# Attention, first of eight layers: TensorE's steps taken in groups, late loads cut in pieces, a normalization started earlier

## The chip, the cores and the metric

The kernel runs on one core of a Trainium2 chip. The metric is device microseconds (us) of one execution; the kernel before has a median of 3373.56 us over three runs (3370.95 to 3374.28). TensorE is called PE in the profile, VectorE DVE, ScalarE ACT, GpSimd POOL and SyncE SP.

## The reference, cut to what matters

The model has eight layers; only the first, a causal attention with 16 heads of 64 features on 4 batches of 1024 tokens and 128 features, is touched. All is in float32.

```
q = split_heads(x @ Wq); k = split_heads(x @ Wk); v = split_heads(x @ Wv)
scores = einsum('bhid,bhjd->bhij', q * beta, k)
scores = where(causal, mask_value, scores)
attn = softmax(scores, axis=-1)
out = einsum('bhij,bhjd->bhid', attn, v)
return out @ Wo + bo
...
x = x + _L0_attn_a_ref(_layernorm(x, axis=-1), ...)
```

## The kernel before, in words

Class `AttentionA` does this layer. Two heads make a pair; pair n (0 to 31) is a batch n // 8 and a pair n % 8 in it. The 1024 queries of a pair are cut in four quarters gq = 0 to 3 of 256 queries, that is two row blocks of 128. Work has two stages, which run about half a pair apart.

The first stage, `probabilities` (lines 336 to 391), takes one row block ib of a quarter at a time, in chunks of up to 512 keys. PE makes the scores of both heads (L352: the heads lie in the two halves of the 64-row weights) into a PSUM tile s. DVE adds the mask, negates, moves the chunk to p in SBUF and keeps the running minimum (L358, one instruction per head). After the last chunk ACT takes the exponential of the block in place (L367, one per head) and sums it. After the second block of a quarter DVE takes reciprocals r (L380), SP stores them to DRAM (L383) and loads them back twice, spread over 64 partitions each (L386), as the tile share.

The second stage, `outputs` (L414), works through a quarter in gq + 1 steps of two key blocks. PE turns the blocks of p with 8 transposes (6 in the last, diagonal step) into PSUM tiles t (L426); DVE copies the first key block to SBUF (L433), ACT the second (L431). Then PE multiplies the turned blocks with v into a PSUM tile o (L451); the two heads go to the two halves of its columns. At the end of a quarter DVE multiplies o with share (L458).

What PE does is written in one fixed order (`pe`, a chain of dependencies over all its instructions of the layer), and DVE's masked minima and the normalization are in another (`ve`). In a step of the kernel before the order is: transposes of this step; one entry of the list `pieces`, if there is one; the scores that `ahead` gives (it keeps the first stage 20 units of 128x128 keys per head ahead of the second); the products of the step **before** (the list `waiting`). Pieces are: two transposes of the normalized x per batch (L260), q and k of a pair (four of L280), values of two pairs (four of L291), the product with Wo (two of L318), and at the end of a batch two transposes back (L328). Each takes the one PSUM tile of the pool `a_pm`, and is evacuated by DVE or ACT.

PSUM has eight banks: two tiles s of two banks each, two tiles t of one, one for o, one for the pieces.

`normalized(b)` (L248) does the layernorm of a batch: on DVE 8 `bn_stats`, 8 `bn_aggr`, a reciprocal and 8 subtract-multiply instructions (L117 to L124), on ACT a square root (L121), on POOL the bias added to x (L251); then it puts the two transposes into `pieces`. It is called for batch b at quarter 0 of pair 8b - 2.

`load_late` (L91) defers the two 2 MB loads of the expert weights W1 and W2 of the second layer; they are issued on ACT's queue, with a small exponential of another layer ahead of them, all at once after the first exponentials of quarter 2 of pair 0 (L371 to L377).

Of the kernel before, what the change touches and what calls it, by code (L numbers as in the profile page):

```python
# [11 lines left out]
F32 = mybir.dt.float32  # L12
# [15 lines left out]
DH_A = 64  # L28
# [33 lines left out]
class Kernel:  # L62
# [28 lines left out]
    def load_late(self, pool, name, shape, src):  # L91

        t = pool.tile(shape, F32, name="w_" + name)
        self.late.append(lambda: self.nc.scalar.dma_start(t, src))
        return t

    def broadcast_row(self, pool, name, width):
# [97 lines left out]
class AttentionA:  # L195
# [8 lines left out]

    Q = 2
    NQ = NC // 2
    LEAD = 20

    def __init__(self, k: Kernel):
# [9 lines left out]
    def __call__(self, start=None):  # L221
# [4 lines left out]
        with self.stack as ctx:  # L226
# [1 line left out]
            one = ctx.enter_context(tc.tile_pool(name="a_one", bufs=1))  # L228
            sb = ctx.enter_context(tc.tile_pool(name="a_sb", bufs=2))
            dram = ctx.enter_context(tc.tile_pool(name="a_dram", bufs=6, space=DRAM))  # L230
            ps_s = ctx.enter_context(tc.tile_pool(name="a_ps", bufs=2, space=PSUM))
            ps_t = ctx.enter_context(tc.tile_pool(name="a_pt", bufs=2, space=PSUM))
            ps_o = ctx.enter_context(tc.tile_pool(name="a_po", bufs=1, space=PSUM))
            ps_m = ctx.enter_context(tc.tile_pool(name="a_pm", bufs=1, space=PSUM))
            pe, ve = k.order(), k.order()
# [6 lines left out]
                out=mask[:, MW - P :], in_=mask[:, MW - P :], compare_op=ALU.is_ge, fill=MASKED, base=0,  # L242
                pattern=[[-1, P]], channel_multiplier=1,
            )
            xts, pairs, units = {}, {}, {}
            pieces = []

            def normalized(b):  # L248
                xl = one.tile([P, NC, C], F32, tag="xl", name="xl")
                k.normalize(xl, k.xb(b), pin=ve)  # L250
                nc.gpsimd.tensor_tensor(  # L251
                    k.xb(b), k.xb(b), bo.unsqueeze(1).to_broadcast([P, NC, C]), ALU.add
                )

                def turned(h):
                    if h == 0:
                        xts[b] = one.tile([P, T], F32, tag="xt", name="xt")
                    ps = ps_m.tile([P, 512], F32, tag="m", name="ps")
                    for c in range(4):
                        pe(nc.tensor.transpose(ps[:, c * P : (c + 1) * P], xl[:, h * 4 + c, :], k.ident))  # L260
                    k.evacuate(xts[b][:, h * 512 : (h + 1) * 512], ps)

                pieces.extend([(NP * b, lambda: turned(0)), (NP * b, lambda: turned(1))])
# [72 lines left out]
            def probabilities(n, gq):  # L336
# [7 lines left out]
                for i in range(Q):  # L344
                    ib = gq * Q + i
                    width = (ib + 1) * P
                    for at, lo in enumerate(range(0, width, 512)):
                        hi = min(lo + 512, width)
                        s = ps_s.tile([P, 2, 512], F32, tag="s", name="s")
                        for h in range(2):  # L350
                            feats = slice(h * DH_A, (h + 1) * DH_A)
                            pe(nc.tensor.matmul(  # L352
                                s[:, h, : hi - lo], q[feats, ib * P : (ib + 1) * P], kk[feats, lo:hi],
                                start=True, stop=True,
                            ))
                        m = mask[:, MW - hi + lo :] if hi == width else mask[:, : hi - lo]
                        for h in range(2):
                            ve(nc.vector.tensor_tensor_reduce(  # L358
                                p[:, h, i, lo:hi], s[:, h, : hi - lo], m, -1.0, 3.4e38, ALU.add, ALU.min,
                                tops[:, h, i, at : at + 1],  # L360
                            ))
                        if hi < width:
                            yield (hi - lo) // P
                    if width > 512:
                        nc.vector.tensor_tensor(tops[:, :, i, 0], tops[:, :, i, 0], tops[:, :, i, 1], ALU.min)  # L365
                    for h in range(2):
                        exp = nc.scalar.activation(  # L367
                            p[:, h, i, :width], p[:, h, i, :width], AF.Exp, bias=tops[:, h, i, 0:1],
                            scale=-1.0, accum_out=sums[:, h, i : i + 1],
                        )  # L370
                    if k.late and gq == 2:  # L371
                        pin = k.order()
                        pin(exp)
                        while k.late:
                            pin(k.late.pop(0)())
                        while k.late_v:
                            ve(k.late_v.pop(0)())  # L377
                    if i == Q - 1:
                        r = sb.tile([P, 2, Q], F32, tag="r", name="r")
                        nc.vector.reciprocal(r, sums)  # L380

                        there = dram.tile([2, Q, P], F32, tag="shares", name="shares")
                        nc.sync.dma_start(there.rearrange("h i p -> p h i"), r)  # L383
                        share = sb.tile([P, Q * P], F32, tag="share", name="share", bufs=4)
                        for h in range(2):
                            nc.sync.dma_start(  # L386
                                share[h * DH_A : (h + 1) * DH_A],
                                there[h : h + 1].rearrange("h i p -> h (i p)").to_broadcast([DH_A, Q * P]),
                            )
                        units[n, gq] = p, share  # L390
                    yield (hi - lo) // P
# [17 lines left out]
                    else:  # L409
                        break  # L410

            waiting = []

            def outputs(n, gq):  # L414


                p, share = units.pop((n, gq))
                last = (gq + 1) * Q - 1
                for step in range(gq + 1):
                    products = []  # L420
                    for jb in (2 * step, 2 * step + 1):
                        lo = max(0, jb * P - gq * Q * P)
                        t = ps_t.tile([P, 2, Q * P], F32, tag="t", name="t")
                        for h in range(2):
                            for i in range(lo // P, Q):
                                pe(nc.tensor.transpose(  # L426
                                    t[:, h, i * P : (i + 1) * P], p[:, h, i, jb * P : (jb + 1) * P], k.ident
                                ))
                        pt = sb.tile([P, 2, Q * P], F32, tag=f"pt{jb % 2}", name="pt")
                        if jb % 2:  # L430
                            nc.scalar.copy(pt[:, :, lo:], t[:, :, lo:])  # L431
                        else:
                            nc.vector.tensor_copy(pt[:, :, lo:], t[:, :, lo:])  # L433
                        products.append((jb, lo, pt))
                    done[1] += 4 if step < gq else 3
                    if pieces:
                        pieces.pop(0)[1]()
                    ahead()
                    while waiting:
                        waiting.pop(0)()  # L440
                    if step == 0:
                        o = ps_o.tile([P, Q * P], F32, tag="o", name="o")
                    waiting.append(
                        lambda products=products, step=step: product(n, gq, o, share, products, last, step == gq)
                    )

            def product(n, gq, o, share, products, last, at_end):
                for jb, lo, pt in products:
                    for h in range(2):
                        feats = slice(h * DH_A, (h + 1) * DH_A)  # L450
                        pe(nc.tensor.matmul(  # L451
                            o[feats, lo:], pairs[n]["v"][:, jb, feats], pt[:, h, lo:],
                            start=jb == 0, stop=jb == last,
                        ))
                if at_end:
                    if gq == 0:
                        pairs[n]["o"] = sb.tile([P, T], F32, tag="ot", name="ot")
                    nc.vector.tensor_tensor(  # L458
                        pairs[n]["o"][:, gq * Q * P : (gq + 1) * Q * P], o, share, ALU.mult
                    )  # L460

            normalized(0)
            projected(0)
            projected(1)
            ahead()
            for n in range(B * NP):
                for gq in range(NQ):
                    if gq == 0 and n + 2 < B * NP and (n + 2) % NP == 0:
                        normalized((n + 2) // NP)
                    if gq == 1 and n > 0:  # L470
                        joined(n - 1)
                    if gq == 3 and n + 2 < B * NP:
                        projected(n + 2)
                    outputs(n, gq)
            while waiting:
                waiting.pop(0)()
            joined(B * NP - 1)
            while pieces:
                pieces.pop(0)[1]()
# [1354 lines left out]
```

## Time and profile before

| | us |
|---|---|
| median of three runs | 3373.56 |
| the profiled execution | 3378.53 |
| its span, first to last instruction | 3376.7 |
| first layer: first transpose of probabilities to last product with Wo | 31.96 to 1223 |
| PE busy over the span | 3015.2 (89%) |
| DVE busy | 2306.0 (68%) |
| ACT busy | 1812.9 (54%) |
| mean granted PE clock | 0.947 |

The page gives, for each engine, the time in which it worked; groups of instructions by line; and a chain of waits. In the timeline each row is a run of like instructions: start, length, engine, line, what is written from what, number. A matrix product in float32 is two instructions there, a transpose one. Lengths of PE rows overlap by the time a result is under way, so the distance from one row's start to the next row's start is what PE takes for it.

### The profile page before, as it was taken

The numbers are of one execution on the slowest core, as the hardware profiler recorded it, in microseconds if no ns is written. First come the engines' busy times: TensorE is split into PE (matmuls) and PEld (weight loads), VectorE is DVE, ScalarE is ACT, GpSimd is POOL, SyncE is SP. The second block draws the span as 40 slices with busy tenths as digits, with TensorE's granted clock in tenths as the row PEclk, the third lists the DMA queues.
The fourth block names the chain that finished last, engine by engine and source line by source line (L and its number), as shares of the span: only waits on it lengthen the run. The fifth ranks groups of instructions, "written<-read, shape, count | busy, mean of one in ns | idle before, by whom it ended". The sixth has DMA issues, their size and how long they took to land.

```text
span 3376.7 us, 45533 instructions
## 1 busy us (share of the span) xinstructions
PE 3015.2 (89%) x16624; PEld 1655.0 (49%) x16624; DVE 2306.0 (68%) x5281; ACT 1812.9 (54%) x3819; POOL 273.0 (8%) x269
## 2 busy tenths in 40 slices
PE   5999999999999979869988597978778799999988
PEld 2555555555455547635566344444445344444435
DVE  3666666666776656666566589897977677677634
ACT  2555555555555523445423597979654265556662
POOL 1000000000000002530013200000001101010000
PEclk8999999999999989989999798989999699899999
DMA  5110111111110101100001111111111112121100
GB/s 156 16 16 14 15 18 16 14 17 17 14 17 15 15 8 32 53 10 1 0 16 40 53 64 50 57 57 51 63 38 42 34 44 53 31 51 31 30 2 25
DMA packets 149537, 109.35 MB, mean 32 GB/s; under 512 B 91760, under 2 KB 130432, under 8 KB 146880
## 3 DMA queue, kind: packets, MB, share of 16 engines
q1 hardware_dynamic: 128352, 72.84, 9.4%
q0 software_dynamic: 17408, 27.32, 3.3%
q10 hardware_dynamic: 3552, 6.29, 0.6%
q8 instruction: 130, 2.13, 0.4%
q14 instruction: 95, 0.78, 0.1%
HBM read 90.76 MB, written 15.60 MB: 31 GB/s over the span
## 4 chain that ended last, share of the span: by engine, by line
PE 68%; DVE 11%; ACT 8%; DMA 6%; issue 6%; POOL 1%; SPq 0%; DVEq 0%; ACTq 0%; POOLq 0%
PE s L352 8%; PE t L426 8%; PE o L451 8%; PE acc L649 4%; PE o L1613 4%; PE acc L1227 4%; PE x L1579 3%; PE ps L280 3%; PE acc L948 3%; PE s L1515 3%; ACT p L1585 3%; DMA shares<-r 2%; ACT hc L1226 2%; DVE st L1214 2%; DVE tops L1524 2%
## 5 line engine op out<-in xcount | busy, mean ns | idle before, releaser
L358 DVE CUSTOM_DVE_ANT_0 p<-s,mask 128x512 f32<-128x512 f32 (+3 forms) x768 | 394.6, 553 | 170.5 <-PE s L352 168.3
L367 ACT ACTIVATE p<-p,tops 128x640 f32<-128x640 f32 (+7 forms) x512 | 391.7, 767 | 146.1 <-DVE tops L365 85.4
L1585 ACT ACTIVATE p<-x 128x512 f32<-128x512 f32 (+3 forms) x768 | 337.6, 490 | 246.4 <-PE x L1584 176.6
L1524 DVE TENSOR_REDUCE tops<-s 128x2 f32<-128x1024 f32 (+3 forms) x384 | 361.3, 956 | 133.8 <-PE s L1520 94.2
L431 ACT COPY pt<-t 128x512 f32<-128x512 f32 (+1 forms) x320 | 157.7, 493 | 380.0 <-PE t L426 379.5
L1227 PE MATMUL acc<-hc,ident 128*128 128x512 f32 x512 | 270.1, 652 | 93.2 <-ACT hc L1226 92.3
L352 PE MATMUL s<-kt,qt 64*128 64x512 f32 (+3 forms) x1536 | 339.4, 533 | 2.7 <-DVE tops L358 2.6
L451 PE MATMUL o<-pt,vv 128*64 128x256 f32 (+1 forms) x2560 | 323.3, 374 | 14.7 <-ACT pt L431 9.4
L426 PE MATMUL t<-ident,p 128*128 128x128 f32 x2304 | 326.2, 282 | 3.7 <-DVE pt L433 3.0
L426 PEld LDWEIGHTS t<-ident,p 128*128 128x128 f32 x2304 | 248.1, 142 | 103.3 <-issue 70.0
L1214 DVE TENSOR_TENSOR_SCAN st<-decay,st 128x1024 f32<-128x1024 f32 x128 | 288.8, 2279 | 10.9 <-ACT decay L1211 10.4
L451 PEld LDWEIGHTS o<-pt,vv 128*64 128x64 f32 x2560 | 156.6, 137 | 263.9 <-issue 157.3
L433 DVE COPY pt<-t 128x512 f32<-128x512 f32 x320 | 220.0, 687 | 66.0 <-PE t L426 66.0
L1579 PE MATMUL x<-q,k 75*128 75x512 bf16 (+3 forms) x768 | 223.1, 338 | 27.7 <-ACT p L1585 15.0
L1515 PE MATMUL s<-k,q 72*128 72x512 bf16 (+3 forms) x768 | 216.3, 348 | 31.9 <-DVE tops L1524 17.6
L1226 ACT ACTIVATE hc<-ps,by_time 128x256 f32<-128x256 f32 x512 | 200.7, 478 | 50.6 <-PE ps L1220 50.5
L352 PEld LDWEIGHTS s<-kt,qt 64*128 64x128 f32 x1536 | 112.5, 188 | 180.7 <-issue 139.7
L1227 PEld LDWEIGHTS acc<-hc,ident 128*128 128x128 f32 x512 | 91.7, 198 | 209.6 <-ACT hc L1226 191.0
L738 POOL DMA_INDIRECT got<-y_rows,rows x128 | 136.7, 1068 | 645.1 <-DMA y_rows<-y 543.5
L1213 DVE TENSOR_TENSOR st<-du,bs 128x1024 f32<-128x1024 f32 x128 | 151.8, 1217 | 49.4 <-PE ps L1220 49.2
L649 PE MATMUL acc<-d,xl 128*128 128x480 f32 (+1 forms) x384 | 152.8, 559 | 26.2 <-DVE d L644 26.2
L1220 PEld LDWEIGHTS ps<-ident,st 128*128 128x128 f32 x1024 | 126.0, 146 | 96.5 <-issue 60.7
(272 smaller groups left out, 4740.7 us busy)
## 6 DMA issues: line engine op xcount, KB each, us to landing
bs<-b_rows SPq DMA_DIRECT2D x64, 512.0 KB
share<-shares SPq DMA_DIRECT2D x256, 64.0 KB
k<-b_parts POOLq DMA_DIRECT2D x16, 576.0 KB, 13.2
q<-b_parts POOLq DMA_DIRECT2D x48, 192.0 KB, 12.1
b_parts<-part SPq DMA_DIRECT2D x24, 256.0 KB
y_rows<-y SPq DMA_DIRECT2D x16, 192.0 KB
x<-in_x_dram SPq DMA_DIRECT2D x4, 512.0 KB
w_W<-in_W_dram ACTq DMA_DIRECT2D x1, 2048.0 KB
```

Source lines behind the costliest of these rows:

```text
L352: pe(nc.tensor.matmul(s[:, h, : hi - lo], q[feats, ib * P : (ib + 1) * P], kk[feats, lo:hi], start=True, stop=True,))
L358: ve(nc.vector.tensor_tensor_reduce(p[:, h, i, lo:hi], s[:, h, : hi - lo], m, -1.0, 3.4e38, ALU.add, ALU.min, tops[:, h, i, at : at + 1],))
L367: exp = nc.scalar.activation(p[:, h, i, :width], p[:, h, i, :width], AF.Exp, bias=tops[:, h, i, 0:1], scale=-1.0, accum_out=sums[:, h, i : ...
L426: pe(nc.tensor.transpose(t[:, h, i * P : (i + 1) * P], p[:, h, i, jb * P : (jb + 1) * P], k.ident))
L451: pe(nc.tensor.matmul(o[feats, lo:], pairs[n]["v"][:, jb, feats], pt[:, h, lo:], start=jb == 0, stop=jb == last,))
L649: pe(nc.tensor.matmul(acc[n][:, :m, :].rearrange("p e s -> p (e s)"), xl[:, c, :], d[:, e : e + m, :].rearrange("p e s -> p (e s)"), start ...
L1214: nc.vector.tensor_tensor_scan(st, decay, st, 0.0, ALU.mult, ALU.add)
L1227: nc.tensor.matmul(acc[:, c : c + 2, :].rearrange("p c d -> p (c d)"), k.ident, hc.rearrange("p c d -> p (c d)"), start=n == 0, stop=n == ...
L1515: start.pin(nc.tensor.matmul(s[:, a, : hi - lo], qq[:ROWS, two + a, ib * P : (ib + 1) * P], kk[:ROWS, two + a, lo:hi], start=True, stop=ha ...
L1524: nc.vector.tensor_reduce(tops[:, half, two : two + 2, n], s[:, :, : hi - lo], AX.X, ALU.max)
L1579: start.pin(nc.tensor.matmul(x[:, lo:], kk[:FULL, a, jb * P : (jb + 1) * P], qq[:FULL, a, hq * 512 + lo : (hq + 1) * 512], start=True, sto ...
L1585: nc.scalar.activation(p[:, a, lo:], x[:, lo:], AF.Exp)
```

## The change

Three edits in the first layer.

1. The late loads are cut along the second dimension: W1 and W2 in eight pieces of 256 KB each. Instead of all at once they are issued one per quarter, after the last exponential of the quarter, from quarter 2 of pair 0 on (the small exponential takes the first turn).
2. `normalized` for a batch is called half a pair earlier, at quarter 2 of pair 8b - 3; the two transposes (`across`) are put into `pieces` where they were, at quarter 0 of pair 8b - 2.
3. `outputs` works in groups of steps: quarter 0 has one group of one step, quarter 1 one of two, quarter 2 one of three, quarter 3 two of two. In a group the order is: a piece; all transposes of the group's steps; a piece; the scores that `ahead` gives; the products of this same group. `waiting` is gone. The tiles t of a step are one tile of two banks, taken from the pool of the scores, which now has three tiles for both; the SBUF copies pt have three buffers each instead of two.

```diff
+    GROUPS = [[(0,)], [(0, 1)], [(0, 1, 2)], [(0, 1), (2, 3)]]
...
-        self.late.append(lambda: self.nc.scalar.dma_start(t, src))
+        self.late.extend(
+            lambda at=at: self.nc.scalar.dma_start(t[:, at], src[:, at]) for at in range(shape[1])
+        )
...
-            ps_s = ctx.enter_context(tc.tile_pool(name="a_ps", bufs=2, space=PSUM))
-            ps_t = ctx.enter_context(tc.tile_pool(name="a_pt", bufs=2, space=PSUM))
+            ps_s = ctx.enter_context(tc.tile_pool(name="a_ps", bufs=3, space=PSUM))
...
-                    if k.late and gq == 2:
+                    if k.late and i == Q - 1 and n * NQ + gq > 1:
                         pin = k.order()
                         pin(exp)
-                        while k.late:
-                            pin(k.late.pop(0)())
+                        pin(k.late.pop(0)())
...
+                o = ps_o.tile([P, Q * P], F32, tag="o", name="o")
+                for steps in self.GROUPS[gq]:
+                    piece()
+                    blocks = [block for step in steps for block in turned(p, gq, step)]
+                    piece()
                     ahead()
-                    while waiting:
-                        waiting.pop(0)()
...
+                    for block in blocks:
+                        product(n, gq, o, *block)
...
+                t = ps_s.tile([P, 2, 2, Q * P], F32, tag="s", name="t")
+                blocks = []
+                for m in range(2):
...
+                    blocks.append((jb, lo, sb.tile([P, 2, Q * P], F32, tag=f"pt{m}", name="pt", bufs=3)))
+                for m, (jb, lo, pt) in enumerate(blocks):
+                    if m:
+                        nc.scalar.copy(pt[:, :, lo:], t[:, m, :, lo:])
+                    else:
+                        nc.vector.tensor_copy(pt[:, :, lo:], t[:, m, :, lo:])
+                done[1] += 4 if step < gq else 3
+                return blocks
...
+                    if gq == 2 and n + 3 < B * NP and (n + 3) % NP == 0:
+                        normalized((n + 3) // NP)
                     if gq == 0 and n + 2 < B * NP and (n + 2) % NP == 0:
-                        normalized((n + 2) // NP)
+                        across((n + 2) // NP)
```

More of the change, by code (lines that the diff above doesn't have):

```diff
@@ L244, in __call__ @@
             )
-            xts, pairs, units = {}, {}, {}
+            xls, xts, pairs, units = [], {}, {}, {}
             pieces = []
@@ L253, in normalized, with across @@
                 )
+                xls.append(xl)
+            def across(b):
+                xl = xls.pop()
                 def turned(h):
@@ L410, in ahead, with piece @@
                         break
-            waiting = []
+            def piece():
+                if pieces:
+                    pieces.pop(0)[1]()
             def outputs(n, gq):
                 p, share = units.pop((n, gq))
[L418 to L437, printed above, removed]
-                    ahead()
-                    while waiting:
-                        waiting.pop(0)()
[L441 to L445, printed above, removed]
@@ L447, in product @@
-            def product(n, gq, o, share, products, last, at_end):
-                for jb, lo, pt in products:
-                    for h in range(2):
[L450 to L460, printed above, removed]
+                o = ps_o.tile([P, Q * P], F32, tag="o", name="o")
@@ new lines, in outputs @@
+                for steps in self.GROUPS[gq]:
+                    piece()
+                    blocks = [block for step in steps for block in turned(p, gq, step)]
+                    piece()
+                    ahead()
+                    for block in blocks:
+                        product(n, gq, o, *block)
+                if gq == 0:
+                    pairs[n]["o"] = sb.tile([P, T], F32, tag="ot", name="ot")
+                nc.vector.tensor_tensor(
+                    pairs[n]["o"][:, gq * Q * P : (gq + 1) * Q * P], o, share, ALU.mult
+                )
@@ new lines, in turned @@
+            def turned(p, gq, step):
+                t = ps_s.tile([P, 2, 2, Q * P], F32, tag="s", name="t")
+                blocks = []
+                for m in range(2):
+                    jb = 2 * step + m
+                    lo = max(0, jb * P - gq * Q * P)
+                    for h in range(2):
+                        for i in range(lo // P, Q):
+                            pe(nc.tensor.transpose(
+                                t[:, m, h, i * P : (i + 1) * P], p[:, h, i, jb * P : (jb + 1) * P], k.ident
+                            ))
+                    blocks.append((jb, lo, sb.tile([P, 2, Q * P], F32, tag=f"pt{m}", name="pt", bufs=3)))
[6 more added lines that the diff above has]
+                return blocks
@@ L462, in __call__, with product @@
+            def product(n, gq, o, jb, lo, pt):
+                for h in range(2):
+                    feats = slice(h * DH_A, (h + 1) * DH_A)
+                    pe(nc.tensor.matmul(
+                        o[feats, lo:], pairs[n]["v"][:, jb, feats], pt[:, h, lo:],
+                        start=jb == 0, stop=jb == (gq + 1) * Q - 1,
+                    ))
             normalized(0)
+            across(0)
             projected(0)
@@ L474, in __call__ @@
                     outputs(n, gq)
-            while waiting:
-                waiting.pop(0)()
             joined(B * NP - 1)
```

## The prediction

> **What bounds the kernel now.** I read the page first, then busy times by stretch, then PE's timeline inside a stretch, then the waits around the stretches that are not full. The stretch 97 to 281 us (pairs 1 to 5) is the first layer in its steady state:
>
> ```profile
> core 0: us, PE busy (x) PEld busy (x) DVE busy (x) ACT busy (x) POOL busy (x), PEclk, DMA share, GB/s
> 31.00:97.00 66.00, 45.27 (x202) 23.21 (x200) 23.23 (x71) 20.45 (x49) 2.35 (x2) 0.77 0.32 85
> 97.00:281.00 184.00, 184.00 (x1145) 98.64 (x1142) 127.19 (x396) 97.56 (x233) 0.00 (x0) 1.00 0.12 16
> ```
>
> PE is busy for all 184 us at full clock, DVE for 69%, ACT for 53%: here PE alone sets the time. In 31 to 97 us it is busy for 45 of 66 us at a clock of 0.77. So two questions decide: what PE spends beyond its products, and what comes next once that is less. PE's timeline, two cycles:
>
> ```profile
> 330.47 1.13 PE L352 MATMUL s<-kt,qt 64*128 64x512 f32 x4
> 331.53 1.08 PE L451 MATMUL o<-pt,vv 128*64 128x256 f32 x8
> 332.54 1.09 PE L426 MATMUL t<-ident,p 128*128 128x128 f32 x8
> 333.47 1.03 PE L291 MATMUL ps<-w_Wv,xt 128*128 128x256 f32 x4
> 334.43 1.13 PE L352 MATMUL s<-kt,qt 64*128 64x512 f32 x4
> 335.49 0.87 PE L451 MATMUL o<-pt,vv 128*64 128x256 f32 x8
> 336.29 1.09 PE L426 MATMUL t<-ident,p 128*128 128x128 f32 x8
> ```
>
> Read start to start. Scores take 1.06 for 512 keys (330.47 to 331.53), 0.63 for 256 (320.08 to 320.71): 0.213 per 128 keys and 0.20 beside it. Two score chunks in a row (512 and 128, 316.12 to 317.40) take 1.28, so the 0.20 comes once per run, not per chunk. Products take 1.01, or 0.80 when the second block is half: the same 0.213, and 0.16 beside. Eight transposes take 0.93, six 0.71: 0.107 each and 0.07 beside. A piece takes 0.95: 0.853 and 0.10. Without a piece transposes to scores is 1.03 (299.94 to 300.97), so 0.17 instead of 0.07 + 0.10. Each cycle scores, products, transposes thus pays **0.53 us for changing from one form of product to the next**.
>
> Does that close? Per pair, scores, transposes and products are 36 units each way: 3 x 7.68. Odd pairs have 10 pieces, even ones 6, of 0.853. With ten cycles: 23.0 + 8.5 + 5.3 = 36.9 odd, 33.5 even. The chain of waits has 37.0 (96.4 to 133.4) and 33.7 (to 167.1). It closes.
>
> **The groups (edit 3).** Ten cycles per pair become five. A piece ahead of the transposes adds a change of form: products to piece is 0.17 (1214.03 to 1215.69, sixteen product instructions worth 1.49), in place of products to transposes, and piece to transposes I take at 0.09, between the 0.07 and 0.10 that like changes cost. Odd pairs have five such pieces, even ones three: saved 5 x 0.53 - 0.45 = 2.20 and 5 x 0.53 - 0.27 = 2.38, that is 4.6 us per two pairs. Over 31 pairs (the last is tail): **-71 us** (0.09 between 0 and 0.2: -82 to -58).
>
> What covered before and is late now? I wrote out the order that the code gives; an odd pair is, with T for the eight or six transposes of a step, S with its units, O for the products of a step:
>
> ```
> gq0: piece T piece S4 O            gq1: piece T T piece S3 S4 O O
> gq2: piece T T T piece S4 S1 S2 S3 O O O
> gq3: piece T T piece S4 S4 O O     piece T T piece S1 S4 S2 O O
> ```
>
> (a) Four scores in a row in gq2 meet three PSUM tiles: S3 needs the tile of S4. When DVE gives it back, DVE's timeline shows for a chunk of 512 whose row on PE starts at 614.82:
>
> ```profile
> 615.99 0.69 DVE L358 CUSTOM_DVE_ANT_0 p<-s,mask 128x512 f32<-128x512 f32 x1 [0.29 <-PE s L352]
> 616.61 0.08 DVE L358 DVE_READ_ACCUMULATOR2_ANT tops<- 128x1 f32 x1
> 616.61 0.69 DVE L358 CUSTOM_DVE_ANT_0 p<-s,mask 128x512 f32<-128x512 f32 x1
> 617.22 0.08 DVE L358 DVE_READ_ACCUMULATOR2_ANT tops<- 128x1 f32 x1
> ```
>
> DVE is done 2.48 after the score starts; PE would come back after S4, S1, S2 = 1.49. Stall 1.0 us per pair, with O O O behind it: **+31** (0 if the tiles come free otherwise, +40 if DVE is late besides).
>
> (b) Products wait for their own copies instead of the step before's. DVE's copy is ready about 1.5 us after a step's transposes start (0.75 latency, 0.69). With a piece and scores between, 2 us, it is hidden; that covers all groups but gq0 of even pairs, which has no pieces. And ACT's copy stands behind exponentials in ACT's order:
>
> ```profile
> 613.15 0.87 PE L426 MATMUL t<-ident,p 128*128 128x128 f32 x6
> 613.26 0.94 ACT L367 ACTIVATE p<-p,tops 128x768 f32<-128x768 f32 x1 [2.08 <-DVE tops L365]
> ...
> 615.11 0.35 ACT L431 COPY pt<-t 128x256 f32<-128x256 f32 x1
> ```
>
> The copy ends 2.3 us after these transposes start. Before, nobody was waiting; in gq0 of an even pair the products come 0.81 + 1.06 = 1.9 after, with 0.43 of the first block ahead: some 0.3 late, or 1.2 where the reciprocal (L380; 84.1 us of DVE idle ahead of it in the groups by line, all behind ACT and the stores) holds DVE too. I take 0.65 per two pairs, **+10**; ends 0 and 2 us for every pair, +62.
>
> (c) SP: per pair its stores, waits for landings and loads fill 31.8 of 35.7 us (631.98 to 663.75 of 631.98 to 667.72). A pair will take some 34, so SP still fits; under 31.8 it could not go.
>
> **Normalization (edit 2).** Now transposes stand from 280.40 and the next from 285.07:
>
> ```profile
> 280.40 0.87 PE L426 MATMUL t<-ident,p 128*128 128x128 f32 x6
> 285.07 1.24 PE L260 MATMUL ps<-ident,xl 128*128 128x128 f32 x4 [3.79 <-DVE xl L124]
> 286.24 2.08 PE L352 MATMUL s<-kt,qt 64*128 64x512 f32 x4
> ```
>
> From 280.40 to the scores at 290.81 it is 10.4 us for 4.6 of work; the other two are 11.5 and 10.6: 18.8 us lost in three, part as the wait, part as the half clock after it (scores 2.01 instead of 1.06). Moved, the same 25 DVE instructions (1.65 + 0.62 + 0.20 + 2.14 = 4.6 us), ACT's root with 1.28 of table load before and after, and POOL's 2.35 come in gq2 of an odd pair. In `ve` the masked minima queue behind them, so the next scores' tiles and ACT's exponentials are late: DVE has some 11 us idle per pair but not in one place. I take 3 us for each, bounds 1 and 5: **-10** (-16 to -4). The gaps should stay under those that cost the clock here; a gap of 0.66 (before 315.06) left the next scores at full speed (1.28 for 512 and 128 keys).
>
> **Late loads (edit 1).** 31.96 to 96.31 takes 64.4 us; by the rates above it is 33 of work, so 31 lost. ACT stands until 50.28 with one load of W; PE stands from 44.1 to 53.5 for ACT's copy, then 3.2 for share (before 61.39), behind 4 MB of loads, all followed by half clock:
>
> ```profile
> 50.28 0.02 ACT L94 MOVE_SHAPE w_W<-in_W_dram  x1 [17.23 <-DMA w_b<-in_b_dram]
> ...
> 53.52 0.70 PE L451 MATMUL o<-pt,vv 128*64 128x128 f32 x4 [9.42 <-ACT pt L431]
> ```
>
> In pieces the 17.2 goes. Late next is share of gq0, stored at 36.09: alone, store to load takes 8 to 10 us here, so its product wait ends near 48, some 5 us; the four q and k in a row still wait for their evacuation (2.6 + 0.8 + 0.7). I take 13 left, **-18** (-26, to 0 if a piece's issue waits as the W load did). Sixteen issues of 0.38 to 0.88 us are 6 to 14 us of ACT over 17 quarters, beside 47% idle. The expert weights are needed at 1266 us, after the last piece near 190.
>
> The row says a 2 MB load in one hurt. The Trainium skill, "DMA: Bandwidth & Descriptors", section Bandwidth, says the opposite of cutting: batch to at least 1 MiB. By its fit (2 us fixed, 436 GB/s) sixteen pieces are an estimated 28 us more of transfer than two; were that on the path, the total would be about -28 instead of -56. No row here puts it there.
>
> **Tail.** The last share lands 14 us after its reciprocal (1206.2 to 1220.2) and PE waits 4.4 for it; grouping puts the last scores behind 14 transposes more (1.5 us), and products wait for copies with nothing between: **+2** (0 to +4).
>
> **Sum**: -71 + 31 + 10 - 10 - 18 + 2 = -56. The profiled execution goes from 3378.5 to 3322.5; it lies 5.0 above the median, so the median goes from 3373.6 to **3318**.
>
> **Rivals.** *The stalls do not come* (tiles free in time, copies early): (a) and (b) are 0 and the sum is -97: 3277. For it: DVE has 31% idle. Against: the 2.48 above is a chain, not a load. *The stalls are longer*, by half to all of the 41 of (a) and (b) again (reciprocals that block DVE, SP's rounds, late exponentials): 3338 to 3359, middle 3348. *Slower*: products that wait for their own group's copies at every group, behind exponentials in ACT's queue. It gains 71 + 10 + 18 = 99 without stalls; over 155 groups that is eaten from 0.64 us mean stall per group on; at 0.8 it is +25, 3399. For it: the copy's 2.3 us; against: most groups have a piece and up to four scores there, 2 to 3 us. *The 0.53 is paid per step*, not per change: then grouping saves nothing, the sum is +15, 3389; against it, the two chunks in a row.
>
> **Numbers.** Forecast (3300 to 3334) 0.45; stalls do not come (3262 to 3300) 0.24; longer (3334 to 3366) 0.20; within 0.2% (about 7 us, what a measurement here can tell from no change) 0.03; the two slower ones 0.08. The range takes the forecast, most of the second down to 3268 and of the third up to 3352. Faster 0.89, same 0.03, slower 0.08.
>
> **What would show it.** Steady stretch: two pairs in 68 to 69 us instead of 70.7; fives of cycles per pair; S3 of gq2 released by DVE about 1 us late; a few tenths at gq0 of even pairs; no idle at L260; no 17 us wait at L94. Wrong I would be if rows of products wait for copies everywhere, or if transposes in long rows take more than 0.107 each.

## The result, and the profile after

The changed kernel takes 3384.08 us (median of seven runs, 3380.64 to 3393.69) against 3373.56 of the kernel before on the same chip: ratio 1.0039, 95% interval 1.0023 to 1.0055. It is 0.4% slower; the forecast was 3318. The profiled execution of after has a span of 3387.2 us at a granted clock of 0.943 (before 3376.7 at 0.947).

The busy times by stretch, first layer of after. Columns as named in the first line:

```profile
core 0: us, PE busy (x) PEld busy (x) DVE busy (x) ACT busy (x) POOL busy (x), PEclk, DMA share, GB/s
31.00:97.00 66.00, 49.70 (x288) 29.10 (x284) 32.45 (x105) 27.05 (x63) 2.33 (x2) 0.90 0.25 38
97.00:281.00 184.00, 167.53 (x1070) 99.33 (x1071) 123.81 (x394) 97.24 (x224) 2.35 (x1) 0.98 0.20 32
```

The start got better: DVE is busy 32 of 66 us in place of 23, the clock is 0.90 in place of 0.77. But in the steady stretch PE, which was busy without a gap, now stands for 16.5 of 184 us. In the same time PE gets less done there (1070 instructions in place of 1145), because it waits.

PE's timeline in after: first the place where the moved normalization holds DVE, then the transposes of the normalized batch, then the four scores of a gq2, then half of a gq3:

```profile
258.12 1.78 PE L359 MATMUL s<-kt,qt 64*128 64x512 f32 x12
262.57 0.92 PE L359 MATMUL s<-kt,qt 64*128 64x384 f32 x4 [2.67 <-DVE tops L365]
...
280.34 0.66 PE L267 MATMUL ps<-ident,xl 128*128 128x128 f32 x4
280.83 0.82 PE L450 MATMUL t<-ident,p 128*128 128x128 f32 x6
...
624.04 1.78 PE L359 MATMUL s<-kt,qt 64*128 64x512 f32 x12
626.58 0.92 PE L359 MATMUL s<-kt,qt 64*128 64x384 f32 x4 [0.76 <-DVE tops L365]
...
646.29 1.13 PE L359 MATMUL s<-kt,qt 64*128 64x512 f32 x4
647.35 1.08 PE L465 MATMUL o<-pt,vv 128*64 128x256 f32 x8
648.36 1.13 PE L325 MATMUL ps<-ot,w_Wo 128*128 128x512 f32 x2
649.32 1.69 PE L450 MATMUL t<-ident,p 128*128 128x128 f32 x14
```

What the prediction named is there. The wait of 3.8 us ahead of the normalization's transposes is gone (280.34 has none), and one of 2.67 stands at the earlier place. The fourth score of a gq2 starts 2.54 us after the first (624.04 to 626.58), with 1.49 of work between: it is 1.05 late, of which the profile shows 0.76 as idle, since the rows overlap. Two quiet pairs, an odd and an even one, take 36.25 + 32.51 = 68.8 us in place of 36.35 + 34.37 = 70.7. Over the page, scores, products and transposes are busy 97 us less (339.4 to 317.1, 323.3 to 295.6, 326.2 to 279.4).

But not all pairs are quiet. Start of the last evacuation `ot` of a pair, and the time since that of the pair before:

| pair | before: end (took) | after: end (took) |
|---|---|---|
| 0 | 106.0 | 85.0 |
| 1 | 142.3 (36.3) | 132.0 (47.1) |
| 3 | 213.1 (36.4) | 207.9 (40.6) |
| 6 | 325.8 (36.2) | 320.9 (40.4) |
| 17 | 725.1 (36.4) | 715.3 (36.3) |
| 18 | 759.5 (34.4) | 756.3 (41.1) |
| 29 | 1160.4 (36.4) | 1156.2 (36.2) |
| 30 | 1191.7 (31.4) | 1193.5 (37.3) |
| 31 | 1220.2 (28.4) | 1230.3 (36.7) |

The start gains 21 us; the quiet pairs gain a few more; single pairs and the last two give all of it back, and 10 more. The other seven layers keep that difference. One of the places where it goes, in the timeline of after (all engines, other rows left out):

```profile
1181.34 0.42 DVE L437 TENSOR_TENSOR ot<-o,share 128x256 f32<-128x256 f32 x1 [7.33 <-DMA share<-shares]
1181.77 1.26 DVE L458 COPY pt<-t 128x512 f32<-128x512 f32 x2
...
1182.46 1.18 ACT L456 COPY pt<-t 128x512 f32<-128x512 f32 x2 [6.09 <-DVE pt L458]
...
1183.10 2.08 PE L359 MATMUL s<-kt,qt 64*128 64x512 f32 x4 [5.85 <-ACT pt L456]
```

Read from below: PE waits 5.85 us for a PSUM tile that ACT has not yet copied; ACT waits for DVE; DVE stands in `ot`, 7.33 us, for the share's load to land. PE's row names ACT, and the cause is a DMA three steps away. Summed over 100 to 1180 us (us in total, times, longest), DVE's two waits on the share's trip in after:

```profile
DVE ot L437 <- DMA share<-shares: 52.5, 21, 8.5
DVE r L386 <- DMA shares<-r: 51.0, 27, 3.6
```

In the kernel before, the first has at most 16.2 us over the whole layer (its group by line, last column: idle before it), and the second 34.3 in the same stretch:

```profile
L458 DVE TENSOR_TENSOR ot<-o,share 128x256 f32<-128x256 f32 x128 | 53.7, 420 | 16.4 <-DMA share<-shares 16.2 <-PE o L451 0.2
DVE r L380 <- DMA shares<-r: 34.3, 19, 3.8
```

### The profile page after: what moved, and what is told of

Its sections match the earlier page's. It is cut to its first block, busy times and chain, and to the rows that moved or that the text cites. A ratio compares the mean times of both kernels' runs of the same rounds, so it can differ in the third digit from the quotient of the medians.

```text
span 3387.2 us, 45418 instructions
## 1 busy us (share of the span) xinstructions
PE 2972.4 (88%) x16624; PEld 1700.7 (50%) x16624; DVE 2313.1 (68%) x5281; ACT 1826.9 (54%) x3820; POOL 272.0 (8%) x269
## 5 line engine op out<-in xcount | busy, mean ns | idle before, releaser
L359 PE MATMUL s<-kt,qt 64*128 64x512 f32 (+3 forms) x1536 | 317.1, 529 | 64.2 <-ACT pt L456 36.7
L1223 DVE TENSOR_TENSOR_SCAN st<-decay,st 128x1024 f32<-128x1024 f32 x128 | 288.7, 2278 | 10.9 <-ACT decay L1220 10.3
L465 PE MATMUL o<-pt,vv 128*64 128x256 f32 (+1 forms) x2560 | 295.6, 372 | 0.2
L450 PEld LDWEIGHTS t<-ident,p 128*128 128x128 f32 x2304 | 259.0, 141 | 57.5 <-issue 42.3
L450 PE MATMUL t<-ident,p 128*128 128x128 f32 x2304 | 279.4, 273 | 0.0
L465 PEld LDWEIGHTS o<-pt,vv 128*64 128x64 f32 x2560 | 171.7, 139 | 182.3 <-issue 97.9
L359 PEld LDWEIGHTS s<-kt,qt 64*128 64x128 f32 x1536 | 126.7, 192 | 229.4 <-ACT pt L456 75.8
## 6 DMA issues: line engine op xcount, KB each, us to landing
k<-b_parts POOLq DMA_DIRECT2D x16, 576.0 KB, 12.9
```

The source lines that it names most:

```text
L359: pe(nc.tensor.matmul(s[:, h, : hi - lo], q[feats, ib * P : (ib + 1) * P], kk[feats, lo:hi], start=True, stop=True,))
L450: pe(nc.tensor.transpose(t[:, m, h, i * P : (i + 1) * P], p[:, h, i, jb * P : (jb + 1) * P], k.ident))
L465: pe(nc.tensor.matmul(o[feats, lo:], pairs[n]["v"][:, jb, feats], pt[:, h, lo:], start=jb == 0, stop=jb == (gq + 1) * Q - 1,))
L1223: nc.vector.tensor_tensor_scan(st, decay, st, 0.0, ALU.mult, ALU.add)
```

## The theory and its rival

**Theory.** The share's trip took the gain back. For each quarter ("unit", 128 in all) DVE takes the reciprocals, SP stores 512 elements of 4 bytes, waits for them to land, and issues two loads; then DVE multiplies `o` by the share. SP's timeline in after:

```profile
672.74 4.26 SPq L392 DMA_DIRECT2D share<-shares  x4
677.10 0.53 SPq L389 DMA_DIRECT2D shares<-r  x1
687.29 1.08 SPq L392 DMA_DIRECT2D share<-shares  x2
688.43 0.58 SPq L389 DMA_DIRECT2D shares<-r  x1
696.63 1.09 SPq L392 DMA_DIRECT2D share<-shares  x2
700.58 0.36 SPq L389 DMA_DIRECT2D shares<-r  x1
```

A store at 677.10, its loads not before 687.29: 10 us in which SP's queue does nothing else, and the next store, whose reciprocals were done at 681.47, goes out at 688.43. The change makes this worse: the groups bring a quarter's products one cycle forward with respect to the scores, so there is less time between reciprocals and use. The number of rounds (stores, landing, loads) is not what differs: in both traces a pair has three, and pair 1 four. But a store now goes out 2.2 us after its reciprocals in the median, where it was 0.1. Of the units 4 to 119:

| | reciprocals to `ot` (median) | reciprocals to end of the loads' issue (median; 9th tenth) | left until `ot` (median; 1st tenth) |
|---|---|---|---|
| before | 22.9 | 11.3; 13.9 | 11.2; 7.9 |
| after | 17.8 | 11.6; 16.4 | 5.1; 3.0 |

The last column has to cover the loads' landing. In after `ot` waits for the share 26 times. In 14 of them it starts 2.1 to 3.7 us after the end of the loads' issue; in the other 12, which make the long waits, 6.9 to 10.3 us, and in each of these SP had issued the next store within 1.4 us behind the loads (for the wait above: loads at 1171.92 and 1172.42, store at 1174.04, `ot` at 1181.34). Late landings are not new: by the semaphore records of the traces, the loads of 15 of these 116 units landed more than 6 us after the end of their issue in before (at most 9.4), and of 15 in after (at most 10.1). What is new is that they are no longer covered. Before had 7.9 us or more left for nine units in ten; after has 5.1 in the middle.

**Rival.** The groups' own waits did it: the fourth score's and, above all, ACT's copy, which in after starts when DVE's copy of the same tile ends (before, both ran side by side).

## The experiments

The four groups of experiments below ran on four chips, on which the kernel before took 3386.6, 3414.1, 3383.0 and 3400.0 us; ratios are against it on the same chip. The "layer" is the time of the last `ot` of pair 31 in the trace (before 1220.2, after 1230.3). These traces come from different chips, but quiet pairs of like kernels agree on all of them to a tenth (36.3 and 34.4 us in before, e_norm, b_const and b_none).

### Each edit alone

`e_loads`, `e_norm` and `e_groups` are the kernel before with one of the three edits as in the diff; `e_pool` is after with the two loads issued by POOL:

```
-                            nc.sync.dma_start(
+                            nc.gpsimd.dma_start(
                                 share[h * DH_A : (h + 1) * DH_A],
```

> The kernel before with edit 1 alone (W1 and W2 in sixteen pieces, one per quarter). Theory (the share's round trip on SP's queue is what the changed kernel waits for; the pieces only help the start): the first pair ends some 20 us earlier as it does in the changed kernel, SP has room in the kernel before, and most of that is kept: 3352 to 3362 us. Rival (the pieces themselves disturb the share's transfers over the first pairs, pair 1 of the changed kernel having taken 47 us): what the first pair gains is given back by pair 4, 3368 to 3380.

> The kernel before with edit 2 alone (normalization half a pair earlier, its transposes where they were). Theory: PE's three waits of 3.8 us and the half clock after them go, and the masked minima behind the normalization lose 1 to 3 us each time: 3358 to 3368. Rival (the normalization in DVE's order costs more there than it did, as the pairs 5, 6, 13, 14, 21, 22 of the changed kernel suggest, 38 to 41 us each): 3374 to 3390.

> The kernel before with edit 3 alone (groups). Theory: undisturbed pairs take 34.4 instead of 35.4, but SP's round trips fill a pair wholly, the product with share waits for them several times, and the tail is about 10 us longer: 3370 to 3385. Rival (the groups pay their 71 us and the loss comes from edits 1 and 2): 3320 to 3345.

> The changed kernel with the two loads of share issued by POOL instead of SP, so that a store of reciprocals no longer waits on the queue behind the loads of the quarter before. Theory: stores go as soon as the reciprocals are there, the waits of DVE's product with share nearly vanish after the first pair, and what the groups save is seen: 3310 to 3335. Rival (products that wait for their own group's copies, copies one after the other, the fourth score): the round trip is not the cause, 3375 to 3390.

Measured: e_loads 3409.08, ratio 1.0064 (1.0043 to 1.0085); e_norm 3403.17, 1.0049 (1.0033 to 1.0065); e_groups 3443.21, 1.0178 (1.0148 to 1.0207); e_pool 3640.96, 1.0759 (1.0735 to 1.0783). Every edit alone costs time, 0.5 to 1.8%. e_loads ends its first pair 11 us earlier (94.7) and then has pairs of 39.9, 48.0, 38.8, 44.5: its stores go out one by one (109.46, 122.09, 134.31, 145.43; pairs 1, 2 and 4 have four rounds), and the reciprocals wait for r's two buffers, 71.3 us in place of 34.3. e_norm gains a little in pairs 5, 13 and 21 (41.5, 40.4, 40.8 for 42.2, 42.4, 43.4) and loses more in 6, 14 and 22 (44.1, 46.4, 38.4 for 36.2, 36.1, 35.7): in 6 and 14 a store stands behind the loads of the unit before it, a fourth round. e_groups has a few quiet pairs of 36.25 and 32.5, and others of 40 to 48, with three rounds in every pair; its `ot` waits for the share 117.7 us in 100 to 1180.

e_pool was meant as a remedy and is none. The stores go out at once, but now POOL issues a unit's loads right beside the store of a later unit, and `ot` starts 9.1 to 12.9 us after the end of their issue in 32 of the 33 units in which it waits for the share. The trip gets longer, and with it the kernel; the group by line:

```profile
L437 DVE TENSOR_TENSOR ot<-o,share 128x256 f32<-128x256 f32 x128 | 54.2, 424 | 284.5 <-DMA share<-shares 258.6 <-PE o L465 23.9
```

So a longer trip does set the pace. That a shorter one frees it isn't shown yet.

### A constant in place of the share, and the store on another queue

a_const and b_const leave out the softmax's normalization: `ot` is multiplied by a constant, and nothing reads the share.

```
-                    pairs[n]["o"][:, gq * Q * P : (gq + 1) * Q * P], o, share, ALU.mult
+                    pairs[n]["o"][:, gq * Q * P : (gq + 1) * Q * P], o, flat.to_broadcast([P, Q * P]), ALU.mult
```

That is the edit for a_const (after) and b_const (before); for a_act and b_act the store goes to ACT's queue, written behind the next step's exponentials:

```
-                        nc.sync.dma_start(there.rearrange("h i p -> p h i"), r)
...
+                pin = k.order()
+                pin(last_exp[0])
+                pin(nc.scalar.dma_start(there.rearrange("h i p -> p h i"), r))
```

> The kernel after, with the outputs' evacuation multiplying by a constant 0.01 (one element for each partition, broadcast) in place of the share. Stores, landings and loads of the shares still run on SP, but nothing reads what they bring: the softmax's normalization is left out. Theory (the share's round trip is what took the gain back): pairs then run undisturbed, 36.25 and 32.5 us in turn as in the kernel's quiet stretches, the first layer ends 50 to 75 us earlier than in the kernel after (1230.3 in its trace), and the kernel takes 3305 to 3340. Rival (the groups' own waits, the fourth score in a row and the copies of the two halves, took it back): the gaps behind a late copy stay, and the time is within 15 us of the kernel after, 3370 to 3390.

> The control: the kernel before with the same constant in place of the share (the softmax's normalization is left out). Theory: in the kernel before the share came in time in nearly all pairs (16.4 us of waits in 128 evacuations), so only 5 to 20 us go: 3353 to 3369; the difference to the kernel after with the constant is then the change without the share, 30 to 60 us in the change's favour. Rival: as much goes as with the kernel after (50 us or more), and the share bounds both alike.

> The kernel after, all of its computation kept, with the share's store issued by ACT's queue, written behind the exponentials of the next step, so that ACT doesn't wait for the reciprocal; the two loads stay on SP, which now only waits for landings, and a store no longer stands behind the loads of the unit before it. Theory: the three or four rounds of store, landing and loads on one queue are gone, the loads follow their store by 9 to 10 us each for itself, the share is there 5 us or more ahead of its use, and most of the 50 to 75 us come back: 3315 to 3350. ACT pays some 0.1 us of issue 128 times and isn't the bound. If the rate of rounds isn't the cause but only the lead, less comes: 3350 to 3380. Rival (the groups' own waits): 3380 or more, as the store takes ACT time ahead of the copies.

> The control: the kernel before with the store on ACT's queue in the same way. Theory: before's pairs had room for three rounds on SP, so little goes: 0 to 15 us faster, 3358 to 3374, and the changed kernel with the store on ACT stands 20 to 50 us ahead of it. Rival: the kernel before gains as much as the kernel after does.

Measured: a_const 3393.70, ratio 0.9944 (0.9924 to 0.9964), layer 1211.9; b_const 3400.09, 0.9964 (0.9947 to 0.9981), layer 1214.8; a_act 3565.30, 1.0441 (1.0397 to 1.0486); b_act 3449.82, 1.0113 (1.0076 to 1.0150).

a_const was a miss for the theory as it was put: it gained 18 us in the layer, not 50 to 75, and it is hardly ahead of b_const. Its waits (100 to 1180 us) say why the test wasn't clean:

```profile
DVE r L388 <- DMA shares<-r: 103.3, 29, 7.7
```

Nothing reads the share any more, but r has two buffers, each held until its store has landed: the trip still stops DVE, one instruction earlier than before, and twice as long as in after (51.0). Taking away one reader of a slow transfer moved the wait to its other end.

a_act missed on the other side. No store waits behind SP's loads any more, but behind the next exponentials it goes out up to 7.9 us after the reciprocals (9th tenth), the loads are issued up to 19.1 us after them, and DVE's `ot` waits 161.8 us in 100 to 1180, three times as long as in after. So it is no rate of rounds on SP alone; what counts is the time from the reciprocals to the share, however it comes about. b_act, with 23.6 us between reciprocals and use (median; a_act 20.0), loses a quarter as much.

### No trip, and a short one

a_none and b_none are after and before with the constant, and without store and loads; the softmax's normalization is left out there too. a_turned and b_turned keep all of the computation and shorten the trip: DVE turns the reciprocals in blocks of 32 x 32, so that 16 pieces of 128 bytes are stored in place of 512 of 4. The turned tile lies in the columns of p that the unit's first row block leaves free, so r has no buffers to wait for.

```
-                        r = sb.tile([P, 2, Q], F32, tag="r", name="r")
-                        nc.vector.reciprocal(r, sums)
+                        nc.vector.reciprocal(upright[:, : 2 * Q], sums.rearrange("p h i -> p (h i)"))
+                        free = (gq * Q + 1) * P
+                        r = p[:, 1, 0, free : free + 32]
+                        nc.vector.transpose(r, upright)
...
-                        nc.sync.dma_start(there.rearrange("h i p -> p h i"), r)
+                        for at in range(2 * Q):
+                            nc.sync.dma_start(
+                                there[at // Q, at % Q].rearrange("(b p) -> b p", p=32), r[at::32]
+                            )
```

> The kernel after with a constant in place of the share and without the share's store and loads; the reciprocals stay, and nothing reads them (the softmax's normalization is left out). With the constant alone the first layer of the kernel after ended at 1211.9 us, but DVE's reciprocals still waited 103 us for the buffer of r, that is for the store two units earlier to land, so the round trip still paced DVE. Theory (the round trip, by either wait, is what took the gain back): without it the reciprocal waits for nothing, the pairs take 36.25 and 32.5 us in turn (39 at the moved normalization), the first layer ends at 1165 to 1195, and the kernel takes 35 to 65 us less than the kernel after. Rival (the groups' own waits): it ends where it ended with the constant, 1205 to 1215, 15 to 20 us less than the kernel after.

> The control: the kernel before with the constant and without store and loads (the softmax's normalization is left out). Theory: before's pairs had room for the round trip; as with the constant alone its first layer ends at 1205 to 1216, 5 to 15 us less than the kernel before, so that the changed kernel without the round trip stands 25 to 50 us ahead of it. Rival: it ends as early as the changed kernel does without the round trip, and the groups of steps bring nothing of themselves.

> The kernel after, all of its computation kept, with the reciprocals turned on DVE before they are stored: a transpose of [128,32] in blocks of 32 x 32 lays the four columns of r in rows of 32, and four stores with 4 rows of 128 bytes each (16 pieces of 128 bytes in place of 512 of 4 bytes) take the place of one. The turned tile lies in the part of p that the unit's first step doesn't use, so r has no buffers to wait for. Theory: pieces, not issues, make the landing of 8 to 10 us; it falls to 2 to 4 us, a round on SP to some 6 to 7 us (four stores of 0.4 us, the landing, two loads of 0.5 us), the shares are there 5 us or more ahead of the outputs, and the kernel takes 30 to 60 us less than the kernel after. If the landing has a fixed cost and doesn't fall, the round gets longer by three issues, and it takes 20 to 60 us more than the kernel after.

> The control: the kernel before with the same turned store. Theory: it gains little, 0 to 15 us, since its pairs had room for the round trip; the changed kernel with the turned store stands 20 to 50 us ahead of it and is faster than both kernels. Rival: both gain the same.

Measured:

| | median us | ratio to before (95%) | layer ends |
|---|---|---|---|
| a_none | 3302.18 | 0.9760 (0.9738 to 0.9781) | 1140.4 |
| b_none | 3352.94 | 0.9897 (0.9867 to 0.9927) | 1199.4 |
| a_turned | 3299.63 | 0.9755 (0.9730 to 0.9780) | 1144.0 |
| b_turned | 3347.57 | 0.9893 (0.9866 to 0.9920) | 1192.2 |

The theory holds and the rival falls. The groups' waits are in a_none and a_turned as well, and with the trip gone or short these end the layer 86 to 90 us earlier than after does, more than expected. **a_turned beats both kernels**: 2.45% less than before, with the reference's whole computation. Its page, and the group of `ot`:

```profile
PE 2937.7 (89%) x16624; PEld 1689.4 (51%) x16624; DVE 2344.1 (71%) x5410; ACT 1826.6 (56%) x3820; POOL 272.4 (8%) x269
L444 DVE TENSOR_TENSOR ot<-o,share 128x256 f32<-128x256 f32 x128 | 54.1, 423 | 15.1 <-PE o L472 7.3 <-DMA share<-shares 3.4 <-issue 0.3
```

`ot` waits 3.4 us for the share in place of 83.0 in the whole layer. The trip of one unit, on DVE and on SP:

```profile
637.89 0.17 DVE L387 RECIPROCAL upright<-sums 128x4 f32<-128x4 f32 x1
638.09 0.21 DVE L390 STREAM_TRANSPOSE p<-upright 128x32 f32<-128x32 f32 x1
```

```profile
638.33 2.12 SPq L394 DMA_DIRECT2D shares<-p  x4
640.54 1.47 SPq L399 DMA_DIRECT2D share<-shares  x2
```

Four stores go out in 2.1 us, and by the end of the last one the first loads can go. From the reciprocals to the end of the loads' issue it is 5.1 us (median) in place of 11.6, and 12.3 us are left until `ot`. The price is 0.21 us of DVE and three issues on SP per unit.

The controls missed their expectation: before gains 30 us (b_none) and 35 (b_turned), where 0 to 15 was expected. In b_turned the first pair ends at 91.3 in place of 106.0 and the last two pairs take 51.7 us in place of 59.8; at the end, and perhaps at the start, before was bound by the trip too.

### Each edit alone, with the short trip

t_loads, t_norm and t_groups are e_loads, e_norm and e_groups with the turned store of b_turned.

> The kernel before with the turned store and with edit 1 alone (the late loads in sixteen pieces behind the exponentials of later units). Alone, without the turned store, the edit cost 0.6 per cent. If that loss was the round trip's (stores left unpaired on SP behind loads), the first pair now ends 10 to 18 us earlier than in the kernel before with the turned store (91.3), the later pairs are its own, and the kernel stands at 0.983 to 0.987 of the kernel before, against 0.9893 without the edit. If the pieces have a cost of their own (their issue on ACT, their traffic), pairs 1 to 5 are longer than 36.7 and 34.0 us again and it stands at 0.991 or more.

> The kernel before with the turned store and with edit 2 alone (the normalization two units earlier, its transposes left where they were). Alone it cost 0.5 per cent. If that was the fourth round on SP, the pairs 5 and 6, 13 and 14, 21 and 22 now take 2 to 4 us less together than 42.2 and 35.0, and the kernel stands at 0.985 to 0.989 of the kernel before; if the moved normalization delays DVE's minima by more than it spares TensorE, at 0.990 to 0.995.

> The kernel before with the turned store and with edit 3 alone (groups of steps, one kind of work written after the other). Alone it cost 1.8 per cent. The prediction's step for it was 71 us less by fewer changes of form, 41 us more by the fourth score's and the copies' waits, 30 us less in all. If the loss was the round trip's, the pairs take 36.25 and 32.5 us, and the kernel stands at 0.978 to 0.983 of the kernel before. If the groups have waits of their own that only the turned store together with the other edits hides, at 0.987 or more.

Measured: t_loads 3371.22, ratio 0.9918 (0.9901 to 0.9934); t_norm 3364.03, 0.9897 (0.9873 to 0.9921); t_groups 3345.73, 0.9838 (0.9822 to 0.9855); without an edit 0.9893. The layer's end shows more than the totals, since the chips differ. Against its own base (before 1220.2, b_turned 1192.2):

| edit | with the long trip | with the short trip | as predicted |
|---|---|---|---|
| 1, late loads | +34.4 | -2.3 | -18 |
| 2, normalization | +16.1 | +0.4 | -10 |
| 3, groups | +60.3 | -26.6 | -28, with the tail |
| all three | +10.1 | -48.2 | -56 |

All three losses were the trip's. t_groups meets its expectation in the trace (36.25 and 32.51) and misses its ratio by a little. t_loads and t_norm bring next to nothing in total: t_loads lands in its other case, though its pairs are b_turned's but for some tenths in 2, 5, 6 and 14; t_norm lies between its two. The sum of the singles is -28.5, of all three -48.2. From t_groups to a_turned, where edits 1 and 2 come to the groups, it is -21.6 in two terms: the first pair ends 8.6 us earlier (85.05 to 76.41), and the pairs around the normalization (5 and 6, 13 and 14, 21 and 22) gain 5.1, 3.5 and 4.5. So with groups, edit 2 brings 13.0, without them 6.5 (2.9, 1.8, 1.8). What hides 6.5 in t_norm is its first pair, 98.2 against 91.3, in which it doesn't differ from b_turned. The end of the first pair scatters: it differs by 5.5 us between before and e_norm too (106.0 and 100.5), whose edit doesn't touch it. So edit 1's part is known to no better than 5 to 7 us, and neither are the two small numbers of the table.

## Why the prediction was wrong, point by point

- **What bounds the kernel.** PE alone in the quiet pairs of before: right. For the last two pairs it was not enough, as b_turned shows (51.7 us in place of 59.8).
- **The cost of a change of form, and edit 3's -71.** Nearly right. Two pairs were to take 68 to 69 us, and a_turned has 36.25 + 32.51 = 68.8 in eight of the fourteen twos of pairs 1 to 28; the other six lie at the batches' ends. That is 2.0 less than 70.7, with 2.1 of (a) in it: some 4.1 saved by fewer changes, where 4.6 were forecast. Alone with the short trip, edit 3 brings 26.6 us where 28 were predicted, tail included.
- **(a), +31.** Right in place, mechanism and size: in 26 of 31 pairs of a_turned the fourth score of gq2 starts 2.54 us after the first, with 1.49 of work between, 1.05 late each. The profile's idle time for these waits is less (27.1 us in all with the normalization's), since the rows before them overlap the wait.
- **(b), +10.** Smaller: 2.9 us of waits for ACT's copy in a_turned. That ACT's copy now follows DVE's was not foreseen, and it cost nothing that could be seen.
- **(c), "SP still fits": this step failed.** It was priced at nothing and cost 58 us: the layer of after ends 86.3 us behind that of a_turned, that of before 28.0 behind b_turned. Counted from the end of the first pair, which scatters, it is 64, and by a_none and b_none 66. The 31.8 of 35.7 us were read off one pair with three rounds. A row that the prediction cites under (b) held the hint: of the 84.1 us of DVE's idle time ahead of L380, 36.8 are waits for a store to land, so the trip stopped DVE in before already. The step asked whether the queue has room on the mean. It did not ask how late each share would be: edit 3, by the prediction's own written order, moves the products of a quarter one cycle ahead of where they were, 5 us, and a trip of 11.6 us at the median and 16.4 in the slow tenth, with 2 to 10 us of landing behind it, had 17.8 left in place of 22.9. Nor did it ask whether edits 1 and 2 leave the order of stores and loads on SP as it was: each alone brought a fourth round to two pairs. In after the rounds are as many as before (97 in the layer): what it lost is the lead.
- **Edit 2, -10.** -13.0 with the groups and the short trip. The new wait of 2.67 us stands where it was put and lies inside the bounds of 1 and 5; start to start the scores there take 4.45 us (258.12 to 262.57) for the 2.54 of a quiet pair, so 1.9 of it is the normalization's. Alone with the long trip, the moved work cost a fourth round in two of its three places.
- **Edit 1, -18.** The wait of 17 us at L94 is gone, but behind it stood more than the 5 us seen for the share: in after DVE waits 9.43 us for a store of reciprocals to land (before 45.94), and PE 9.57 for DVE (before 51.05). The first pair gains 5 to 9 us with the short trip, and the pieces cost 3 us again later; with the long trip the gain of 21 us at the start is there in after, and pair 1 gives half of it back. Of the 28 us more of transfer, estimated beside the sum, no more than these 3 are seen.
- **Tail, +2.** The last two pairs take 54.3 us in a_turned and 51.7 in b_turned: +2.6.
- **Rivals.** The stalls "longer" by "SP's rounds" named the right queue and gave it 20 to 41 us. The slower rival had the right sign and the wrong mechanism: products don't wait for copies; copies wait behind `ot`.

Open: how the 58 us divide between `ot`'s own waits and r's two buffers. Each delays the other, and no run took away one alone without moving the wait to the other. Nor was it tried to keep the trip as it is and to start the scores further ahead; that needs a second buffer for the last quarter's probabilities, 16 KB per partition.

## What to carry to other kernels

When a change makes the bounding engine's order tighter, list every transfer that runs beside it, and compare the time from its source to its use with the length of its trip, landing included, in the slow tenth and not at the mean; a queue with room on the mean says nothing of that. When PE's row names a copy, follow that copy's own wait, and so on to the end, before the copy is blamed. And when a small transfer turns out to be in the way, look at its shape first: here two DVE instructions in place of one and a few more issues made a 0.4% loss a 2.45% gain.

## What the runs showed of the hardware that was not expected

- A store of 2 KB in 512 pieces of 4 bytes was followed by its loads 8.4 us later (median over units 4 to 119, in before and in after); as 16 pieces of 128 bytes in four stores, after 0.1 us behind the last issue, 1.3 at most. By the packet records the last of the 512 pieces starts 1.0 us after the end of the issue (median), the last of the 16 pieces 0.7; what comes late is the last signal of the landing, 8.4 us after the end of the issue in after, 8.2 in before, 1.0 in a_turned. The Trainium skill, "DMA: Bandwidth & Descriptors", section Rules for kernel authors, says that a last dimension which isn't contiguous becomes one descriptor per element, and that it should be rearranged to be contiguous; the runs agree and put 2.8% of this kernel's time on it (1.0039 against 0.9755). The same page's section Anatomy of one DMA gives, for DMAs issued by GpSimd, a fixed cost of about 2 us and a term in bytes alone; these stores, issued by SP, had the same bytes and landed 7 us apart, and no run issues such a store from GpSimd. Whether the number of pieces or their 4 bytes make the difference, no run tells.
- A 64 KB load of the share landed 2.0 us after the end of its issue in the best case, and often much later with a store of 512 small pieces issued beside it. With such a store within 1.4 us behind, 15 of 71 units of before and 14 of 73 of after took more than 6 us; of the other units none of 45, and one of 43. In e_pool, where the store is issued 0.25 us ahead of the loads, `ot` starts 9.1 to 12.9 us after them. In a_turned, whose stores have 16 pieces, no load took more than 3.0 us, though 57 of 116 had a store as close behind. The load's own bytes are not what is late: for the wait of 7.33 us above, its packets had run by 1175.74, and 14 of the 16 signals of the second load had come by 1177.02, the last two at 1180.67 and 1181.22. What decides which units are hit stays open.
- A DVE transpose of [128,32] in blocks of 32 x 32 took 0.21 us, 128 times, with 3.2 us of DVE's idle time ahead of all of them together.
